# Scores of narrow attention heads on four row strips at once, and a list planner whose passes use eight settings

## The chip, the core and the metric

The kernel runs on one core of one Trainium2 chip. The core has five engines with a queue each: PE (TensorE, the matrix engine; its weight loads are shown apart as PEld), DVE (VectorE), ACT (ScalarE), POOL (GpSimd) and SP (SyncE, which here only issues DMAs). PE writes to PSUM, which has eight banks; DVE and ACT read them. The metric is the device time of one execution in microseconds (us), as the median of several runs.

## The reference, cut to what matters

Four layers run one after another on x, 16 sequences of 128 tokens of width 128, with a context of 16 x 77 tokens of width 96. Each layer is a gated cross attention and a gated feed-forward, both on a normalised x:

```python
x = x + tanh(g_xattn[l]) * xattn_l(layernorm(x), ctx_768)
x = x + tanh(g_ffn[l]) * ffn_l(layernorm(x))
```

The attention of layers 0 and 3 has 16 heads of width 8 (here: the narrow heads):

```python
q = (x @ wq + bq).reshape(B, Sq, 16, 8).transpose(0, 2, 1, 3)
k = (y @ wk + bk).reshape(B, -1, 16, 8).transpose(0, 2, 1, 3)
scores = einsum('bhqd,bhkd->bhqk', q, k) / sqrt(8)
out = einsum('bhqk,bhkd->bhqd', softmax(scores), v)
```

Layer 1 has 16 heads of width 64 (the wide heads), layer 2 one head. The feed-forward of layers 0 and 2 sends each token to two, and to one, of eight experts; that of layer 1 mixes eight linear experts; that of layer 3 has ternary weights.

## The kernel before, in words

**Tiling.** The 16 sequences are four groups of four (GB = 4 batches of a group). Everything is float32; a float32 matmul shows as two passes of PE in a profile, a transpose as one.

**Narrow heads** (`narrow_heads`, line 847). A group gets its keys (a matmul), spreads them with a mask over 128 partitions into `kk`, 32 rows for each strip of four heads, and gets `q` by a projection. Then, for each of four batches: 16 heads are four strips of 32 rows. Two strips write one score tile (`sc_tile`: two PSUM banks), so a batch has two score tiles (`hf` 0 and 1), each from one pair of matmuls of 32 rows by 308 columns. For each tile DVE takes the maximum of each head (`mx_a<-banks`, a reduction) and subtracts it (`shared<-banks,mx_a`), ACT takes the exponential, and PE transposes the result (12 transposes into three banks, copied out by DVE or ACT). Matmuls of 32 columns multiply it with the values; others make the sums, and after four batches the residual x is updated. The values come over DRAM (`all_v`) and are masked on POOL.

**Experts.** After the attention of layers 0 and 2, two groups at a time make a half (`route_half`): DVE ranks the experts, two small matmuls count (`r_seen_f`, `g_sel_f`), DVE computes row indices (`idx_f`), POOL scatters the normalised rows with indirect DMAs (`sorted_x`), SP reads them back in expert order, PE runs the experts tile by tile (`sorted_experts`), and POOL gathers the results (`sorted_y`).

**What sets the order.** No engine's queue is written by hand. Every operation is recorded with an estimated cost, its dependencies and its tiles (`Program.record`); a block `with nc.together(us)` joins several into one operation that is placed as a whole, with all its tiles. `arrange` (line 456) then makes list passes: `forward` takes, step by step, the operation with the smallest start plus weighted cost, under a look-ahead (`ahead`), a weight for old operations (`bias`), a weight of DVE's time (`busy`) and a lead for DMAs (`lead`); `place` gives it PSUM banks and pages and holds back `reserve` of them for older operations; `backward` makes the priorities for the next pass. The pass whose modelled length is shortest is emitted, and each engine executes its part strictly in that order. Copies out of PSUM that either DVE or ACT can make (`nc.either`) get their engine there too. Since all operations are issued from one place, nearly all have line L540 in the profile; tiles tell them apart. `shared` is the common SBUF buffer and `banks` is PSUM.

Of the kernel before, what the change touches and what calls it, by code (L numbers as in the profile page):

```python
# [19 lines left out]
B, S, D = 16, 128, 128  # L20
# [7 lines left out]
PK = 4 * SK  # L28
# [42 lines left out]
class Tile_:  # L71


    def __init__(self, tag, shape, dtype, name, nth):
        self.tag, self.shape, self.dtype, self.name, self.nth = tag, tuple(shape), dtype, name, nth
        self.free = int(np.prod(shape[1:]))
        self.users, self.seen, self.real, self.slot = [], [], None, None
# [135 lines left out]
        self.kept.clear()  # L213


class Program:
    LAG = {"tensor": 0.25, "vector": 0.08, "scalar": 0.08, "gpsimd": 0.1, "sync": 0.1}
    RATE = 290e3
# [2 lines left out]

    PAGE = {"sbuf": 64, "psum": 512}

    def __init__(self, nc, tc, slots, pages, shared, reserve):


        self.nc, self.tc, self.slots, self.reserve = nc, tc, slots, reserve
        self.pages, self.shared = pages, shared
        self.ops, self.count, self.joined, self.shift = [], {}, None, 0
        for e in ("tensor", "vector", "scalar", "gpsimd", "sync"):  # L230
            setattr(self, e, _Engine(self, e))
        self.either = _Engine(self, "vector", "scalar")
        self.spare = _Engine(self, "vector", "gpsimd")
# [219 lines left out]
            op.latest = length - ends[n]  # L453
        return sorted(range(len(ops)), key=lambda n: (-ends[n], n))

    def arrange(self, rounds=7, ahead=800, bias=0.0027, busy=0.33, lead=7.6):

        ops = self.ops
        self.back = [[] for _ in ops]
        for op in ops:  # L460
            for d in op.deps:
                self.back[d].append(op.n)
        order, best = sorted(range(len(ops)), key=lambda n: ops[n].order), None
        for _ in range(rounds):
            length = self.forward(order, ahead, bias, busy, lead)
            if length is None:
                break
            if best is None or length < best[0]:
                places = {t: t.slot for op in ops for t in op.tiles}
                best = length, [(op.start, op.end, op.engine) for op in ops], places  # L470
            order = self.backward()
        assert best is not None, "no room for any tile"
        self.length, times, places = best
        for op, (op.start, op.end, op.engine) in zip(ops, times):
            pass
        for t, t.slot in places.items():
            pass
        return sorted(ops, key=lambda op: (op.start, op.n))
# [116 lines left out]
def tile_gated_blocks(  # L595
# [4 lines left out]
    psum = ctx.enter_context(tc.tile_pool(name="psum", bufs=1, space=PSUM))  # L600

    slots = {
        "mv": 4, "st": 6, "ve": 4, "rstd": 4, "mx": 6, "rs1": 5, "rs2": 4, "off": 4,
    }
# [4 lines left out]
        **{tag: ("sbuf", True) for tag in ("large", "kk", "heads1", "heads2", "we1_sb")},  # L609
    }  # L610
    pages = {"sbuf": 680, "psum": 8}
    nc = Program(tc.nc, tc, slots, pages, shared, {"sbuf": 0, "psum": 1})

    class Tiles:
        def tile(self, shape, dtype=F32, tag=None, name=None):
# [231 lines left out]
    def narrow_heads(layer, wqo, wkv, bq, row, t, groups):  # L847
        for g in groups:
            n = f"a{layer}_{g}"

            mm = mm_tile(f"k_ps_{n}")
            nc.tensor.matmul(mm[:, :GK], lhsT=wkv[: DC + 1, :D], rhs=ctx_of(g), start=True, stop=True)
            kr = sb.tile([P, GB, SK], F32, tag="middle", name=f"kr_{n}")
            evac(kr, mm[:, :GK].rearrange("p (b j) -> p b j", b=GB))
            kk = sb.tile([P, GB, 4, SK], F32, tag="kk", name=f"kk_{n}")
            shape = [P, GB, 4, SK]
            nc.gpsimd.tensor_tensor(
                kk,
                kr[:, :, None, :].to_broadcast(shape),
                col("hmask")[:, None, :, None].to_broadcast(shape),  # L860
                ALU.mult,
            )
            send_narrow_values(g, wkv[: DC + 1, D : 2 * D], n)
            vbs = narrow_values(g, n)
            xnT = transposed(layernorm(g, n), n)
            add_row(g, row)
            q = q_proj(xnT, wqo[:, :D], bq, n)
            oT = sb.tile([P, GB, S], F32, tag="middle", name=f"oT_{n}")
            av, all_chunks = mm_tile(f"av_{n}"), []
            for b in range(GB):  # L870
                scs = [sc_tile(f"sc_{n}_{b}_{hf}") for hf in range(2)]
                for hf in range(2):
                    with nc.together(0.72):
                        for i in range(2):
                            r = 32 * (2 * hf + i)
                            nc.tensor.matmul(
                                scs[hf][:, i, :PK],
                                lhsT=q[r : r + 32, b * S : (b + 1) * S],
                                rhs=kk[r : r + 32, b, :, :].rearrange("p h j -> p (h j)"),
                                start=True,  # L880
                                stop=True,
                            )
                ats, chunks = [], []
                for hf in range(2):
                    scores = scs[hf][:, :, :PK].rearrange("p a (h j) -> p a h j", h=4)
                    at = probabilities(scores, 8, 8.0**-0.5, f"{n}_{b}_{hf}")
                    ats.append(at.rearrange("p r j -> p (r j)"))
                for c in range(3):
                    m = min(CH, PK - c * CH)
                    tp = tp_tile(f"aT_ps_{n}_{b}_{c}")  # L890
                    with nc.together():
                        for k in range(4):
                            at = PK * (k % 2) + c * CH
                            nc.tensor.transpose(tp[:m, k, :], ats[k // 2][:, at : at + m], ident)
                    aT = sb.tile([m, 4, P], F32, tag="middle", name=f"aT_{n}_{b}_{c}")
                    evac(aT, tp[:m])
                    chunks.append(aT)
                avs = av.rearrange("p (b s) -> p b s", b=GB)
                with nc.together(0.8):
                    for c in range(3):  # L900
                        for k in range(4):
                            a = chunks[c][:, k, :]
                            nc.tensor.matmul(
                                avs[32 * k : 32 * k + 32, b, :],
                                lhsT=vbs[b][: a.shape[0], c, k, :], rhs=a,
                                start=(c == 0), stop=(c == 2),
                            )
                all_chunks.append(chunks)


            sums = mm_tile(f"sums_{n}")[:, :S]
            with nc.together(2.6):
                for b in range(GB):
                    for c in range(3):
                        for k in range(4):
                            a = all_chunks[b][c][:, k, :]
                            nc.tensor.matmul(
                                sums[32 * k : 32 * k + 32], lhsT=own[: a.shape[0], c, b, :], rhs=a,
                                start=(b == c == 0), stop=(b == GB - 1 and c == 2),
                            )  # L920
            rs = sb.tile([P, S], F32, tag="rs", name=f"rs_{n}")
            nc.vector.reciprocal(rs, sums)
            wide = mm_tile(f"wide_{n}")
            for b in range(GB):
                nc.tensor.matmul(
                    wide[:, b * S : (b + 1) * S], lhsT=spread[:, b, :], rhs=rs, start=True, stop=True
                )
            rw = sb.tile([P, GT], F32, tag="middle", name=f"rw_{n}")
            evac(rw, wide)
            nc.vector.tensor_tensor(oT.rearrange("p b s -> p (b s)"), av, rw, ALU.mult)  # L930
            y = mm_tile(f"y_{n}")
            with nc.together():
                for b in range(GB):
                    nc.tensor.matmul(
                        y[:, b * D : (b + 1) * D], lhsT=oT[:, b, :], rhs=wqo[:, D : 2 * D],
                        start=True, stop=True,
                    )
            add_to(xs[g].rearrange("p b d -> p (b d)"), y, t)
# [171 lines left out]
    class Route:  # L1110


        def __init__(self, n, count):
            self.n, self.tiles = n, count
            self.e3, self.e4 = [P, count, NE], [P, count, NE, NE]
            self.tri = col("tri").rearrange("p (e f) -> p e f", e=NE)[:, None].to_broadcast(self.e4)
# [678 lines left out]
```

## Time and profile before

| | before |
|---|---|
| median of 3 runs | 726.56 us (726.46 to 730.62) |
| the profiled execution | 725.84 us |
| its span in the profile | 724.0 us |
| mean granted TensorE clock | 0.929 |
| PE, DVE, ACT, POOL busy | 87%, 67%, 55%, 38% of the span |
| passes of the narrow scores (32x308) | 256, busy 40.7 us together |

The profile is one execution. An engine is busy while an instruction of it runs; matmuls overlap in PE's pipeline, so a busy PE is not a full one. A line of a timeline holds merged instructions: start, length, engine, line, operation, output and inputs, count, and in brackets the idle time before and who ended it. "issue" is an idle time for which the profile shows no wait.

### The profile page before, as it was taken

The numbers are of one execution on the slowest core, as the hardware profiler recorded it, in microseconds if no ns is written. First come the engines' busy times: TensorE is split into PE (matmuls) and PEld (weight loads), VectorE is DVE, ScalarE is ACT, GpSimd is POOL, SyncE is SP. The second block draws the span as 40 slices with busy tenths as digits, with TensorE's granted clock in tenths as the row PEclk, the third lists the DMA queues.
The fourth block names the chain that finished last, engine by engine and source line by source line (L and its number), as shares of the span: only waits on it lengthen the run. The fifth ranks groups of instructions, "written<-read, shape, count | busy, mean of one in ns | idle before, by whom it ended". The sixth has DMA issues, their size and how long they took to land. (4 is left out here: it accounts for less than half of the span.)

```text
span 724.0 us, 14843 instructions
## 1 busy us (share of the span) xinstructions
PE 628.8 (87%) x5280; PEld 498.1 (69%) x5280; DVE 483.4 (67%) x1311; ACT 399.3 (55%) x883; POOL 273.9 (38%) x312
## 2 busy tenths in 40 slices
PE   5899477995699989999999999999657998879995
PEld 3587245785698979648756856987434896646795
DVE  5988955582112487398788888737578826587875
ACT  4766224471455587545656466646334664576853
POOL 6524451407104343077274366104646033421010
PEclk9999776998799999999999999999756999979999
DMA  5212530796429776128016437951201932210001
GB/s 136 83 46 80 163 118 16 251 409 256 128 59 340 242 225 195 47 61 232 2 39 181 135 88 250 324 195 36 65 1 55 306 96 60 73 47 14 1 2 59
DMA packets 103239, 92.62 MB, mean 128 GB/s; under 512 B 6726, under 2 KB 92582, under 8 KB 103166
## 3 DMA queue, kind: packets, MB, share of 16 engines
q1 hardware_dynamic: 97166, 81.28, 35.9%
q0 software_dynamic: 3888, 9.35, 4.1%
q10 hardware_dynamic: 2112, 1.05, 0.6%
q8 instruction: 42, 0.69, 0.4%
q14 instruction: 31, 0.25, 0.1%
HBM read 64.29 MB, written 27.36 MB: 127 GB/s over the span
## 5 line engine op out<-in xcount | busy, mean ns | idle before, releaser
L540 PE MATMUL banks<-shared 128*128 128x128 f32 (+8 forms) x3040 | 363.7, 317 | 28.5 <-issue 14.1
L540 PEld LDWEIGHTS banks<-shared 128*128 128x128 f32 (+5 forms) x3040 | 287.3, 174 | 86.0 <-issue 46.0
L540 ACT COPY shared<-banks 104x512 f32<-104x512 f32 (+8 forms) x244 | 142.6, 613 | 126.0 <-PE banks L540 98.7
L540 PE MATMUL banks<-ident,shared 128*128 128x128 f32 (+3 forms) x829 | 124.6, 294 | 32.6 <-DVE shared L540 13.4
L540 PEld LDWEIGHTS banks<-ident,shared 128*128 128x128 f32 (+3 forms) x829 | 100.0, 144 | 62.3 <-issue 18.6
L540 ACT ACTIVATE shared<-banks,shared 128x128 f32<-128x128 f32 x304 | 85.2, 375 | 67.4 <-PE banks L540 37.2
L540 ACT ACTIVATE shared<-shared 128x616 f32<-128x616 f32 (+1 forms) x100 | 70.5, 709 | 59.8 <-DVE shared L540 55.7
L540 DVE TENSOR_TENSOR shared<-banks,shared 128x128 f32<-128x128 f32 (+1 forms) x84 | 26.7, 326 | 85.0 <-PE banks L540 42.2
L540 DVE TENSOR_TENSOR shared<-banks,mx_a 128x616 f32<-128x616 f32 (+1 forms) x100 | 78.1, 781 | 4.2 <-POOL shared L540 0.2
L540 DVE TENSOR_REDUCE mx_a<-banks 128x8 f32<-128x616 f32 (+1 forms) x100 | 77.4, 774 | 5.1 <-PE banks L540 4.0
L540 POOL DMA_INDIRECT sorted_x<-shared,idx_f x48 | 46.7, 974 | 45.7 <-DVE r_both_f L540 22.8
L540 POOL DMA_INDIRECT shared<-sorted_y,idx_f x48 | 46.4, 966 | 45.7 <-DMA sorted_y<-shared 15.0
L540 POOL TENSOR_TENSOR shared<-shared,mine 104x384 f32<-104x384 f32 x32 | 32.5, 1029 | 61.3 <-DMA shared<-all_v 39.7
L540 DVE COPY shared<-banks 128x512 f32<-128x512 f32 (+8 forms) x40 | 25.7, 653 | 40.2 <-PE banks L540 24.0
L540 POOL TENSOR_TENSOR shared<-shared,rs_a 128x616 f32<-128x616 f32 x32 | 38.6, 1217 | 34.7 <-DVE rs_a L540 18.8
L540 POOL TENSOR_TENSOR rstd_f<-ve_f,nhalf 128x4 f32<-128x4 f32 x16 | 16.4, 1022 | 91.0 <-DVE ve_f L540 63.3
L540 POOL TENSOR_TENSOR x<-x,shared 128x128 f32<-128x128 f32 x64 | 28.6, 454 | 39.1 <-DVE x L540 35.3
L540 PE MATMUL banks<-ctx_sb,shared 96*128 96x308 f32 x128 | 38.4, 427 | 0.6 <-DVE x L540 0.6
L540 PE MATMUL banks<-shared,ctx_sb 96*128 96x512 f32 (+1 forms) x80 | 38.4, 596 | 0.2 <-DVE shared L540 0.2
L540 PEld LDWEIGHTS banks<-ctx_sb,shared 96*128 96x128 f32 x128 | 22.3, 190 | 10.3 <-issue 1.9
L540 POOL TENSOR_TENSOR rstd_a<-ve_a,nhalf 128x4 f32<-128x4 f32 x16 | 16.4, 1029 | 31.1 <-DVE ve_a L540 24.3
L540 ACT ACTIVATE shared<-banks,cols_sb 128x128 f32<-128x128 f32 (+1 forms) x44 | 21.3, 521 | 10.7 <-PE banks L540 5.2
(207 smaller groups left out, 665.4 us busy)
## 6 DMA issues: line engine op xcount, KB each, us to landing
shared<-in_wx SPq DMA_DIRECT2D x60, 578.0 KB
shared<-all_u SPq DMA_DIRECT2D x32, 256.0 KB
shared<-all_v SPq DMA_DIRECT2D x32, 156.0 KB
all_v<-shared SPq DMA_DIRECT2D x32, 154.0 KB
sorted_y<-shared SPq DMA_DIRECT2D x76, 64.0 KB
all_u<-shared SPq DMA_DIRECT2D x14, 308.0 KB
shared<-sorted_x SPq DMA_DIRECT2D x6, 512.0 KB
sorted_x<-shared POOLq DMA_DIRECT2D x2, 1472.0 KB
```

Of the source, the lines that this page charges most:

```text
L540: getattr(engine, f)(*(_real(a) for a in args), **done)
```

## The change

It has two parts. The four strips of a batch become one joined operation over both score tiles, with an estimate of 0.8 us instead of twice 0.72; the arithmetic is the same. And the planner's passes take their settings, with the SBUF pages and PSUM banks held in reserve, from a table of eight rows; before, seven passes had one setting and a reserve of no SBUF pages and one PSUM bank.

```diff
+STEPS = [
+    (400, 0.0011, 0.0, 8.6, 30, 2),
+    (400, 0.001, 0.01, 9.2, 30, 2),
+    (300, 0.0041, 0.59, 9.1, 10, 2),
+    (1000, 0.0024, 0.06, 7.8, 0, 3),
+    (1000, 0.0021, 0, 6.2, 0, 3),
+    (1000, 0.0024, 0.08, 6.1, 0, 3),
+    (1000, 0.0021, 0.06, 4.8, 0, 3),
+    (1000, 0.002, 0.01, 6.3, 0, 3),
+]
...
-    def arrange(self, rounds=7, ahead=800, bias=0.0027, busy=0.33, lead=7.6):
+    def arrange(self):
...
-        for _ in range(rounds):
+        for ahead, bias, busy, lead, *pages in STEPS:
+            self.reserve = dict(zip(("sbuf", "psum"), pages))
             length = self.forward(order, ahead, bias, busy, lead)
...
-    nc = Program(tc.nc, tc, slots, pages, shared, {"sbuf": 0, "psum": 1})
+    nc = Program(tc.nc, tc, slots, pages, shared)
...
                 scs = [sc_tile(f"sc_{n}_{b}_{hf}") for hf in range(2)]
-                for hf in range(2):
-                    with nc.together(0.72):
-                        for i in range(2):
-                            r = 32 * (2 * hf + i)
-                            nc.tensor.matmul(
-                                scs[hf][:, i, :PK],
-                                lhsT=q[r : r + 32, b * S : (b + 1) * S],
-                                rhs=kk[r : r + 32, b, :, :].rearrange("p h j -> p (h j)"),
-                                start=True,
-                                stop=True,
-                            )
+                with nc.together(0.8):
+                    for i in range(4):
+                        r = 32 * i
+                        nc.tensor.matmul(
+                            scs[i // 2][:, i % 2, :PK],
+                            lhsT=q[r : r + 32, b * S : (b + 1) * S],
+                            rhs=kk[r : r + 32, b, :, :].rearrange("p h j -> p (h j)"),
+                            start=True,
+                            stop=True,
+                        )
```

Because the planner orders the whole program, both parts move instructions on every engine, in all four layers.

More of the change, by code (lines that the diff above doesn't have):

```diff
@@ L222, with __init__ @@
     PAGE = {"sbuf": 64, "psum": 512}
-    def __init__(self, nc, tc, slots, pages, shared, reserve):
-        self.nc, self.tc, self.slots, self.reserve = nc, tc, slots, reserve
+    def __init__(self, nc, tc, slots, pages, shared):
+        self.nc, self.tc, self.slots = nc, tc, slots
         self.pages, self.shared = pages, shared
```

## The prediction

> **What bounds the kernel now.** The page first: busy shares, then the 40 slices (18.1 us each).
>
> ```profile
> PE 628.8 (87%) x5280; PEld 498.1 (69%) x5280; DVE 483.4 (67%) x1311; ACT 399.3 (55%) x883; POOL 273.9 (38%) x312
> ...
> PE   5899477995699989999999999999657998879995
> ...
> DVE  5988955582112487398788888737578826587875
> ```
>
> PE leads, but its row has holes (slices 5 to 7, 9 to 11, 28 to 31), and where DVE's row shows 8s and 9s early on, PE is not alone. So the second view is busy time by stage:
>
> ```profile
> 0.00:160.00 160.00, 127.41 (x1453) 94.99 (x1454) 117.71 (x284) 82.43 (x161) 65.78 (x76) 0.91 0.43 140
> 160.00:200.00 40.00, 26.14 (x191) 25.76 (x191) 9.60 (x42) 13.40 (x44) 15.40 (x16) 0.79 0.58 204
> 200.00:500.00 300.00, 290.93 (x1841) 231.98 (x1840) 204.56 (x608) 179.85 (x430) 123.13 (x153) 1.00 0.52 158
> 500.00:560.00 60.00, 39.84 (x211) 29.19 (x210) 42.28 (x122) 22.53 (x47) 34.72 (x34) 0.69 0.14 41
> 600.00:724.00 124.00, 104.49 (x1153) 78.62 (x1152) 88.78 (x216) 74.64 (x130) 28.09 (x28) 0.93 0.13 36
> ```
>
> Columns: stretch, its length, PE, PEld, DVE, ACT, POOL busy, granted clock, DMA share, GB/s. From 200 to 500 us PE is busy 97% at full clock: PE work taken out of there shortens the kernel. Layer 0 (0 to 160), the routing for layer 2 (500 to 560) and layer 3 (600 on) are chains in which DVE is busy 70 to 74% and PE waits. The narrow heads, which the change touches, lie only in these.
>
> Third, how the scores run now, in the timeline of PE (start, length, count):
>
> ```profile
> 32.80 0.79 PE L540 MATMUL banks<-shared 32*128 32x308 f32 x4 [0.42 <-DVE shared L540]
> 33.52 0.65 PE L540 MATMUL banks<-ident,shared 128*104 128x128 f32 x4
> ...
> 94.07 0.81 PE L540 MATMUL banks<-shared 32*128 32x308 f32 x8
> 94.81 3.19 PE L540 MATMUL banks<-shared,own 104*32 104x128 f32 x88
> ```
>
> A matmul has two passes here, so x4 is a pair of strips and x8 all four. A lone pair holds PE 0.72 us (32.80 to 33.52), all four strips 0.74 us (94.07 to 94.81). The strips overlap already whenever two pairs stand next to each other.
>
> Fourth, the largest hole, in POOL's and PE's timelines:
>
> ```profile
> 96.25 1.11 POOL L540 DMA_INDIRECT sorted_x<-shared,idx_f  x1 [5.63 <-DVE r_both_f L540]
> ...
> 111.58 0.96 POOL L540 DMA_INDIRECT sorted_x<-shared,idx_f  x1 [0.31 <-issue]
> 126.43 1.04 POOL L540 TENSOR_TENSOR rstd_f<-ve_f,nhalf 128x4 f32<-128x4 f32 x1 [13.89 <-DVE own_f L540]
> ```
>
> ```profile
> 99.73 0.45 PE L540 MATMUL banks<-shared 104*32 104x128 f32 x6 [0.29 <-issue]
> 100.50 0.42 PE L540 MATMUL banks<-shared 104*32 104x128 f32 x4 [0.32 <-issue]
> 101.22 0.31 PE L540 MATMUL banks<-shared 104*32 104x128 f32 x2 [0.29 <-issue]
> ```
>
> While POOL scatters the first half's rows (96 to 112), PE gets a few instructions every 0.7 us and waits for nothing that is shown; from 97.5 to 115.5 PE is busy 9.8 us of 18 and DVE 3.4. The last three scatters then stand behind a normalisation that waits 13.9 us for DVE.
>
> **The change part by part.** Both programs can be built, so I compare their instruction orders. They have the same matmuls and the same POOL and SP instructions; DVE has 16 more, ACT 14 fewer.
>
> *Four strips.* Before, the order holds 21 adjacent foursomes and 22 lone pairs of scores; after, 32 foursomes. By the two rows above PE goes from 21 x 0.74 + 22 x 0.72 = 31.4 us to 32 x 0.74 = 23.7: 7.7 less. 10 of the lone pairs lie in layer 0 and 12 in layer 3. Upper bound of the gain: the scores' row says 40.7 us busy, waits between passes included, so 40.7 - 23.7 = 17. Lower bound: nothing, where DVE ends the wait. I take 2, as PE is 84% busy after 600 us and the 12 there are 12/2 x 0.70 = 4.2.
>
> *Four banks at once.* Both score tiles must now be free (4 of 8 banks) before the foursome starts; before, half a batch could start as soon as one was. Where the next batch waits for the last subtraction of the batch before, DVE idles for PE's start and the foursome: 0.05 us (the pair at 20.98 starts so long after the subtraction's end at 20.93) plus 0.81, say 0.9. There are 31 such changeovers, so at worst 28 us. DVE's new order stands other work between the batches in most: by the mean rows of that work I count 8 changeovers with less than 0.9 us of it, open by 6.2 us together, 3.3 of them in layer 0. Either tile may also come free one subtraction earlier (1.6 us), then nothing is open: bounds 0 and 28, taken 3. Behind the waiting foursome stand, on PE, the transposes of the batch before.
>
> *New order (the list passes).* The planner tries eight settings instead of seven rounds of one, and everything shifts. What the orders show:
>
> PE between the two routings' counting matmuls (159.8 and 541.9 us now): 14 fewer key matmuls of group 0 in the wide layer (two passes of 308 columns, 0.26 us each: six hold PE from 421.23 to 422.78), because they now stand in layer 0's holes: 14 x 2 x 0.26 = 7.3. 8 fewer expert matmuls at 2 x 0.11 (64 passes take 7.36 us) = 1.8, 4 fewer transposes 0.4, one lone pair 0.7: 10.2 us off the stretch that PE bounds for 300 of 382 us. I take 8; bounds 0 (they push out cover there) and 10.
>
> POOL: the normalisation that held three scatters for 13.9 us now stands second, so 15 scatters run in a row, 15 x 1.26 = 19 us after 96 instead of ending at 132. The rows are read at 137.5 now, and PE is 98% busy from 120 to 160 with other work, so this gives little by itself. But group 2's residual is done before the first index, so the whole attention of group 3 and some wide matmuls of 0.26 to 0.43 us, which need fewer instructions per microsecond, are there to fill the hole from 97.5 to 115.5. Between nothing and 14 us (DVE's idle time there); taken 4, because the same scatters run and PE's instructions may come as slowly again.
>
> DVE: the sum of its instructions by their rows grows from 526.6 to 535.1 us, ACT's falls from 465.8 to 458.8 though it loads its tables 22 times instead of 20 (1.28 us each). Ahead of the first index DVE's sums are equal (87.4). The 8 us arise mostly in the wide layers, where DVE is busy 68%: hidden by PE, 0. If that cover is gone, 8.
>
> Tail: after the first score reduction of layer 3's group 2 DVE has 76 us of work instead of 71, but 56 instead of 60 between the last index and that point, and group 0's feed-forward starts 11 us of DVE work earlier. Net 0, bounds -5 and +5.
>
> Sum on the profiled run (725.8 us: span 724.0 and 1.8 around it): -2 + 3 - 8 - 4 = -11, so 714.8; the median of the runs is 0.7 higher, so 715.5, predicted 715.
>
> **The rivals.**
>
> *Nothing to tell.* The foursomes change nothing since most pairs adjoin, and the planner's new order wins in one hole what it loses in another. For it: 7.7 us of PE lie beside DVE work, and total work is the same. Against: the moved key matmuls. 722 to 733, midpoint 727. The Trainium skill, "TensorEngine Tiling (Array Packing)", PSUM Bottleneck, says that a matmul made faster by tiling leaves the reading of PSUM as the bound. By that rule the four strips are worth 0 here and the forecast 717; the rows agree in part: each score tile costs DVE 0.79 + 0.79 us and PE 0.37.
>
> *Slower: the four banks decide.* If foursomes stall PE's queue until both tiles are free, the 6.2 open us are paid, the same again for the 23 covered changeovers at 0.3 each (7), and DVE's extra 8.4 falls on the path in layers 0 and 3; against it stand the 8 of the middle: +14, 740 (734 to 750). It decides once changeovers cost over 0.5 us on average beyond their cover. For it: DVE is busy 19.0 of 20 us from 20 to 40. Against: the fillers. The same page, PSUM Pressure, says that row tiles must lie in different banks and so raise the pressure; no run here yet shows its price.
>
> *Much faster.* The hole at 97.5 closes nearly whole (-13 instead of -4) and the changeovers cost nothing: 703 (698 to 708).
>
> **How the numbers follow.** Forecast (708 to 719) 0.42, much faster 0.16, nothing to tell 0.24, slower 0.18. One per cent, about what can be told from no change, is 7.3 us, so faster means under 719.3 and slower over 733.8: 0.58, 0.24, 0.18. The range 699 to 735 leaves out most of the slower case and the end of the fast one, 0.2 together; the forecast's own range is 708 to 719.
>
> **What would show it.** The scores' row (256 passes) falls from 40.7 us towards 24 to 28, in groups of 8. DVE's reductions show idle time ended by PE: up to 10 us fits, 20 or more is the slower case. The first scatter still starts near 96 and the sixteenth ends near 117. The hole behind it holds more DVE work than 3.4 us. The second counting matmul comes near 158 to 162, the fourth 8 to 12 us before 542; from there to the end it takes 182 as now. I am wrong if the wide layers last as long as now with 14 key matmuls fewer, or if layer 3 lengthens.

## The result and the profile after

| | before | after |
|---|---|---|
| median of 12 runs each | 728.87 us (726.46 to 730.71) | 722.10 us (718.39 to 727.42) |
| the profiled execution | 725.84 us | 722.32 us |
| its span | 724.0 us | 720.6 us |

The ratio is 0.9918, with a 95% interval from 0.9897 to 0.9939: faster by 6.8 us, or 0.8%, where 1.6 to 1.9% was forecast. The direction and the range hold, the size does not.

The page's first rows and the stages of the kernel after (columns as above; the last stretch is 4 us shorter than it was):

```profile
PE 631.9 (88%) x5280; PEld 500.9 (70%) x5280; DVE 492.7 (68%) x1327; ACT 396.9 (55%) x869; POOL 273.2 (38%) x312
...
PE   5989885997599898999999999999648899889987
...
DVE  4998982565023367698888889845488863698775
```

```profile
0.00:160.00 160.00, 132.76 (x1450) 99.17 (x1451) 113.89 (x275) 81.61 (x149) 64.58 (x76) 0.90 0.46 148
...
200.00:500.00 300.00, 290.01 (x1860) 233.93 (x1859) 212.81 (x629) 173.03 (x421) 126.63 (x159) 0.99 0.55 164
```

DVE has 9 us more work, 8 of them in the wide layers, beside a PE that is as full as before. The hole beside the first half's scatters has not closed: in DVE's row slices 6 to 8 were 5, 5, 5 and are 8, 2, 5, so it lies later (slice 7 is 108 to 126 us). PE's timeline has the counting matmuls of the second and the fourth routing:

```profile
166.89 0.34 PE L556 MATMUL banks<-r_seen_f,ones 128*128 128x72 f32 x2
...
540.68 0.70 PE L556 MATMUL banks<-r_seen_f,ones 128*128 128x72 f32 x2 [3.64 <-DVE r_seen_f L556]
```

Before, these stood at 159.8 and 541.9. So layer 0 takes 7.1 us longer, the stretch from the second to the fourth 8.3 us less (373.8 in place of 382.1), and the rest 2.2 us less (179.9 in place of 182.1). The forecast was right about the middle and wrong about layer 0. This is layer 0's hole, in POOL's, DVE's and PE's timelines:

```profile
100.79 1.11 POOL L556 DMA_INDIRECT sorted_x<-shared,idx_f  x1 [2.80 <-DVE st_f L556]
101.93 1.05 POOL L556 TENSOR_TENSOR rstd_f<-ve_f,nhalf 128x4 f32<-128x4 f32 x1
103.18 1.06 POOL L556 DMA_INDIRECT sorted_x<-shared,idx_f  x1 [0.19 <-issue]
...
121.09 0.96 POOL L556 DMA_INDIRECT sorted_x<-shared,idx_f  x1 [0.30 <-issue]
```

```profile
113.70 0.28 DVE L556 TENSOR_SCALAR bos<-bos,tg 128x128 f32<-128x128 f32 x1
124.54 0.22 DVE L556 COPY gs_f<-banks 128x64 f32<-128x64 f32 x1 [10.57 <-remote]
```

```profile
112.86 0.96 PE L556 MATMUL banks<-route,shared 128*128 128x16 f32 x8
113.76 1.61 PE L556 MATMUL banks<-shared 32*128 32x308 f32 x8
117.81 1.29 PE L556 MATMUL banks<-shared 32*128 32x308 f32 x4 [2.44 <-ACT shared L556]
124.82 1.39 PE L556 MATMUL banks<-shared 32*128 32x308 f32 x4 [5.72 <-DVE gs_f L556]
```

The copy of `gs_f` reads what the `route` matmuls wrote, and these end at 113.8 by PE's rows, yet it starts 10.7 us later, 2.5 us after the last scatter (122.05). "remote" says that the view names no one who released it. PE in its turn waits for DVE with the second half of a foursome. In the kernel before, DVE's last wait there likewise ended 2.4 us after a run of scatters (the run's end at 112.5, then this copy):

```profile
114.95 1.29 DVE L540 COPY shared<-banks 104x512 f32<-104x512 f32 x2 [7.71 <-remote]
```

The trace also records semaphores, the counters by which one engine tells another that it is done. The copy of `gs_f` waits for PE's counter, which rises at 116.72 us and then four times from 124.45 to 124.59. Matched in order, these four belong to matmuls that by PE's rows ended at 113.82 (the last `route` one) to 115.37; without the scatters (below) the same four rises come within 0.1 us of the matmuls' ends. In the kernel before, four rises from 114.87 to 115.04 belong to matmuls that ended from 106.2 to 111.6. So, as far as the match goes, DVE and ACT stand because PE's signals come late, here by up to 10.6 us. It is not complete: of the 17 rises due from 99.6 to 115.4 us three have no record.

The scores' rows, the reductions' before and after and PE's after (busy, mean ns, idle before and who ended it):

```profile
L540 DVE TENSOR_REDUCE mx_a<-banks 128x8 f32<-128x616 f32 (+1 forms) x100 | 77.4, 774 | 5.1 <-PE banks L540 4.0
L556 DVE TENSOR_REDUCE mx_a<-banks 128x8 f32<-128x616 f32 (+1 forms) x100 | 77.4, 774 | 9.9 <-PE banks L556 8.7
```

```profile
L556 PE MATMUL banks<-shared 32*128 32x308 f32 x256 | 35.0, 508 | 11.5 <-DVE gs_f L556 5.7 <-ACT shared L556 3.7 <-DVE shared L556 2.0
```

PE's fell from 40.7 to 35.0, not towards 24 to 28. Passes that wait in the hole count too, but they are the smaller part: without the scatters the row is 32.4. The reductions' idle time ended by PE rose from 4.0 to 8.7.

### The profile page after: what moved, and what is told of

It is laid out like the page before. It is cut to its first block, busy times and chain, and to the rows that moved or that the text cites. A ratio compares the mean times of both kernels' runs of the same rounds, so it can differ in the third digit from the quotient of the medians.

```text
span 720.6 us, 14909 instructions
## 1 busy us (share of the span) xinstructions
PE 631.9 (88%) x5280; PEld 500.9 (70%) x5280; DVE 492.7 (68%) x1327; ACT 396.9 (55%) x869; POOL 273.2 (38%) x312
## 5 line engine op out<-in xcount | busy, mean ns | idle before, releaser
L556 PE MATMUL banks<-shared 128*128 128x128 f32 (+7 forms) x3040 | 366.6, 323 | 53.6 <-issue 15.6
L556 PEld LDWEIGHTS banks<-shared 128*128 128x128 f32 (+4 forms) x3040 | 287.7, 177 | 115.0 <-issue 48.4
L556 ACT COPY shared<-banks 104x512 f32<-104x512 f32 (+9 forms) x234 | 137.5, 610 | 133.5 <-PE banks L556 116.8
L556 PE MATMUL banks<-ident,shared 128*128 128x128 f32 (+3 forms) x829 | 123.0, 295 | 11.7 <-ACT shared L733 3.6
L556 PEld LDWEIGHTS banks<-ident,shared 128*128 128x128 f32 (+3 forms) x829 | 101.0, 146 | 41.4 <-issue 14.5
L556 POOL TENSOR_TENSOR rstd_f<-ve_f,nhalf 128x4 f32<-128x4 f32 x16 | 16.4, 1024 | 134.2 <-DVE ve_f L556 94.1
L556 DVE COPY shared<-banks 104x512 f32<-104x512 f32 (+10 forms) x50 | 33.7, 680 | 26.3 <-PE banks L556 22.2
L556 PE MATMUL banks<-shared,ctx_sb 96*128 96x512 f32 (+1 forms) x80 | 40.9, 632 | 0.1
L556 PE MATMUL banks<-ctx_sb,shared 96*128 96x308 f32 x128 | 36.9, 425 | 0.0
```

The lines of the kernel that those rows point to most:

```text
L556: getattr(engine, f)(*(_real(a) for a in args), **done)
```

## The experiments

Theory after the result: the middle's gain is the moved key matmuls; layer 0 lost because the run of scatters holds the other engines up, whatever work stands ready. Rivals: four banks at once do it; or one of the change's two parts does all. All ratios are against the kernel before, run beside (728.5 to 732.4 us).

**The two parts alone.** First the foursomes with the old seven passes, then the eight settings with the old pairs.

```diff
 strips only:   the kernel before
-                for hf in range(2): with nc.together(0.72): two strips
+                with nc.together(0.8): four strips
 settings only: the kernel after
-                with nc.together(0.8): four strips
+                for hf in range(2): with nc.together(0.72): two strips
```

> The kernel before with the foursomes alone; the planner keeps its seven passes of one setting and its old reserve. My theory is that the strips by themselves are worth at most the 2 us that I gave them, and that a changed order decides the rest: 724 to 734 us against about 729 for the kernel before, the scores' row at 26 to 32 us. If the strips carry the change's gain (rival), about 722. If four banks at once stall the queue of PE (rival), the reductions of the scores show 20 us or more of idle time ended by PE, and the time is 735 or more.

> The kernel after with two pairs of strips in place of each foursome; the planner keeps its eight settings. If the settings bring the gain (theory): 718 to 726 us, and from the second to the fourth counting matmul some 376 us as after the change, or less. If the strips bring it (rival): about 729.

Strips alone: 753.93 us, ratio 1.0328 (1.0271 to 1.0385). Settings alone: 737.81, 1.0130 (1.0070 to 1.0189). The stretch from the second to the fourth counting matmul takes 385 us with the settings alone, not the 376 that I expected. Both are slower than before, and both parts together are faster: there is no gain of a part to be added up, since each variant is a new order of the whole program. The first shows 20.2 us of reductions' idle time ended by PE, which is what I had written down for four banks that stall PE; the split foursomes below speak against that cause, though in another order, so what makes this order slow stays open.

**Without the scatters.** In each kernel's own order, the 16 scatters of layer 0's first half are left out when the program is emitted, so that this half's expert rows stay zero.

```diff
+                op = nc.gpsimd.indirect_dma_start(...)
+                if n == "f0_0":
+                    op.calls.clear()
```

> The kernel after in its own order, without the 16 scatters of layer 0's first half (the expert rows of that half stay zero, so two of the four groups get no expert output from their own rows); every other instruction stands where it stood. If the scatters hold the other engines up (theory), the idle time of 10.6 us before the copy of gs_f goes, the granted clock stays above 0.8 between 100 and 125 us, layer 0 ends 8 to 12 us earlier and the time is 710 to 715 us. If the hole is a chain of the order itself (rival), it stays, and the time is 720 to 724.

> The kernel before in its own order, without the same 16 scatters (the expert rows of layer 0's first half stay zero). If the scatters hold the other engines up (theory): from 97.5 to 115.5 us PE is busy 15 us or more in place of 9.8, and the time falls by 6 to 12 us, to 717 to 723. If both kernels lose the same to the scatters, the difference between this and the kernel after without scatters stays at 7 us; if the kernel after loses more to them, it is 10 or more. Rival, the hole is the order's own: no change, 729.

After without them: 705.82 us, 0.9666 (0.9616 to 0.9716). Before without them: 708.22, 0.9713 (0.9662 to 0.9764). Both gain more than I expected: 16 and 21 us. The stage of the hole, before with and then without scatters (two traces, columns as above):

```profile
96.00:121.00 25.00, 16.66 (x171) 10.01 (x164) 8.82 (x16) 3.93 (x7) 12.63 (x13) 0.66 0.12 41
```

```profile
96.00:121.00 25.00, 24.64 (x474) 21.78 (x471) 19.52 (x50) 12.45 (x23) 2.04 (x2) 1.00 0.34 120
```

The same order, with the same work ready: PE issues 474 passes in place of 171, DVE works 19.5 us in place of 8.8, and the granted clock is 1.00 in place of 0.66. The hole is not the order's. Where the steps come in time (us, one profile each):

| | before | after | before, no scatters | after, no scatters |
|---|---|---|---|---|
| index of half 0 | 95.8 | 100.4 | 96.0 | 100.6 |
| x of group 3 | 138.8 | 146.9 | 123.0 | 133.4 |
| index of half 1 | 163.1 | 170.3 | 147.3 | 156.7 |
| index of layer 2's half 1 | 546.1 | 546.1 | 526.3 | 532.2 |

By these profiles the scatters cost 15.8 us before and 13.6 after up to half 1's index, and without them the new order is 9.4 us later there: layer 0 is longer by itself. Single profiles of one order differ: with plain DMAs in place of the scatters (below) half 1's index of the order after comes at 154.4 and 152.6. So layer 0 is longer by 5 to 9 us, and the stall costs 14 to 18 us after, about as much as before.

**Foursomes apart.** The order after; the second pair of nearly every foursome is issued one PE step later.

```diff
+                if four is not None:          # a foursome
+                    for call in [*late, *op.calls[:2]]:
+                        call(engine)
+                    late, tile = op.calls[2:], four
+                    continue
...
+                if late and op.engine == "tensor":
+                    for call in late:
+                        call(engine)
```

> The kernel after in its own order, but the second pair of strips of nearly every foursome is issued one step of PE later (27 of 32 foursomes become two lone pairs; all else stands as it stood). By the rows of 0.72 us for a lone pair and 0.74 for a foursome this gives PE 27 x 0.70 = 19 us more. My theory, that foursomes save PE time beside work of DVE: 722 to 727 us. If the strips are on the path (rival): 732 or more. If four banks at once hold PE up (rival), lone pairs are faster: 715 to 720, and the reductions' idle time ended by PE falls below the 8.7 us of the kernel after.

738.52 us, 1.0163 (1.0101 to 1.0225), 16.4 above the kernel after: 0.61 us for each of 27 pairs of strips taken apart. PE's row of the scores grows from 35.0 to 54.6 us. Against my theory, the strips are on the path. The reductions now wait more for PE, not less:

```profile
L571 DVE TENSOR_REDUCE mx_a<-banks 128x8 f32<-128x616 f32 (+1 forms) x100 | 77.5, 775 | 17.3 <-PE banks L571 14.8
```

So whatever it costs to need four banks at once, in this order it is less than taking the foursomes apart costs.

**What of a scatter it is.** The same 64 KB each, as plain DMAs from POOL, then from SP.

```diff
+                if n == "f0_0":
+                    op.calls[:] = [lambda engine: engine.dma_start(out=d.rows[at : at + P], in_=xn[:, i, :])]
```

> The kernel after in its own order; the 16 scatters of layer 0's first half become 16 plain DMAs of the same 64 KB from the same queue of POOL (rows go to fixed places, so that half's rows reach the wrong experts). Leaving the scatters out took 16 us. If writing descriptors on POOL is what holds the others up, the hole stays: 718 to 724. If it is the scatter with indices alone, it goes: 706 to 711.

> As the run before, but the 16 plain DMAs stand in the queue of SP. If POOL's part of a scatter holds the others up (theory): the hole goes, 706 to 711 us. If it is the traffic itself (1 MB in 128 pieces of 512 B each), it stays: 718 to 724.

706.95 us (0.9714, 0.9659 to 0.9770) and 708.20 (0.9733, 0.9683 to 0.9783): as without scatters. Neither the megabyte (16 times 128 rows of 512 B) nor POOL's queue does it by itself. What is left is the form with indices, or the long run that it makes: plain ones follow each other every 0.5 us, so that theirs is short.

```profile
100.64 8.03 POOL L1397 DMA_DIRECT2D sorted_x<-shared  x15
```

**Pauses between scatters.** The order after, with a small operation on POOL behind each scatter (first a power of 1.02 us behind all 16, then behind every second, then a short multiplication behind all, then a power behind every fourth); the short one also in the kernel before.

```diff
+                if n == "f0_0":               # or: and k, for every second
+                    op.calls.append(
+                        lambda engine: engine.tensor_tensor(pad[:, :4], pad[:, 4:], pad[:, 4:], ALU.pow)
+                    )
```

> The kernel after with its scatters, but POOL does a small power of 128x4 (1.02 us in the row of rstd_f) after each of the 16 scatters of layer 0's first half, so that they come every 2.4 us in place of 1.27, and end near 140 us. Nothing of the result changes. If the stall comes from scatters that follow each other without a pause, DVE's idle time of 10.6 us before the copy of gs_f falls below 4 and the time is 712 to 719; if each scatter holds the others up by a fixed time (16 us / 16 = 1 us), the hole is only spread, 719 to 725; if the later rows are what matters, 725 or more.

> The kernel after with a 1 us power on POOL after every second scatter of layer 0's first half: the sixteenth ends near 132 us in place of 140 as with 16 powers, so that rstd_f of group 3 and the reading of the rows should not come late. Theory (scatters one after the other without a pause stall PE): if pairs of scatters are still harmless, x3 is updated near 135 us, the second index comes near 159 and the time is 708 to 714. If every pair of scatters already stalls (rival), x3 is updated at 141 or later and the time is 716 to 722.

> The kernel after with a short multiplication (128x128, 0.46 us by the row of x<-x,shared) on POOL after each of the 16 scatters: one every 1.75 us, the sixteenth near 131 us. If a pause of half a microsecond is enough: 708 to 714 us, x3 updated near 135. If the stall goes with the rate of scatters (rival; 1.27 us stalls, 2.3 does not): 714 to 720, x3 near 140.

> The kernel after with a 1 us power after every fourth scatter of layer 0's first half (four powers). If the stall builds up over a long run of scatters without a pause: runs of four are still short, x3 is updated near 133 us and the time is 707 to 712. If it goes with the mean rate (1.27 us stalls, 1.75 does not; here 1.53): x3 at 137 to 142 and 712 to 718.

> The kernel before with the same short multiplication after each scatter of layer 0's first half. There rstd_f of group 2 stands behind thirteen scatters and will come near 119 us; without stalls its inputs are there at 108. If the scatters' rate is what stalls: x2 is updated near 110 to 114 us instead of 123.7, and the time is 718 to 725; the gain is smaller than in the kernel after, whose rstd_f stands second. If pauses do nothing (rival): 728 to 732.

| | us | ratio (95%) | x of group 3 |
|---|---|---|---|
| all 16, 1.02 us | 719.51 | 0.9857 (0.9789 to 0.9925) | 135.0 |
| every second, 1.02 us | 709.39 | 0.9708 (0.9669 to 0.9748) | 133.2 |
| all 16, short | 710.94 | 0.9725 (0.9689 to 0.9761) | 135.1 |
| every fourth, 1.02 us | 711.07 | 0.9734 (0.9701 to 0.9767) | 135.3 |
| before, all 16, short | 720.32 | 0.9856 (0.9817 to 0.9895) | 131.8 |

In the kernel after each pattern brings group 3's x to within 2 us of where it comes without any scatter (133.4), though all scatters are done. POOL and DVE with a pause after every second:

```profile
102.65 0.98 POOL L558 DMA_INDIRECT sorted_x<-shared,idx_f  x1 [0.30 <-issue]
103.65 1.04 POOL L1397 TENSOR_TENSOR pad<-pad 128x4 f32<-128x4 f32 x1
104.89 1.03 POOL L558 DMA_INDIRECT sorted_x<-shared,idx_f  x1 [0.20 <-issue]
```

```profile
111.07 0.22 DVE L558 COPY gs_f<-banks 128x64 f32<-128x64 f32 x1 [0.77 <-PE banks L558]
```

The 10.57 us before the copy are 0.77. With all sixteen long pauses the hole goes as well, but the scatters end at 140 us: DVE then waits 4.06 us for group 3's `rstd_f`, which stands behind them on POOL, and the rows are read 12 us later than in the kernel after (141.65 for 130.03), so the gain is paid back. Runs of four with a pause behind them are nearly harmless there, which fits a stall that builds up over a longer run. In the kernel before, x of group 2 comes at 112.3 us in place of 123.7, and then POOL's queue shows what it waits for:

```profile
117.71 1.01 POOL L542 DMA_INDIRECT sorted_x<-shared,idx_f  x1 [0.17 <-issue]
118.74 0.42 POOL L1382 TENSOR_TENSOR pad<-pad 128x128 f32<-128x128 f32 x1
119.10 1.06 POOL L542 TENSOR_TENSOR rstd_f<-ve_f,nhalf 128x4 f32<-128x4 f32 x1
```

`rstd_f` of group 2 runs with no idle time before it, behind the thirteenth scatter, 6.8 us after that x; without scatters it runs 2.8 us after it (108.6 and 111.4). In the kernel after it stands second.

**The moved key matmuls.** The 14 key matmuls of the wide layer that the new order puts into layer 0 are left out.

```diff
+                if getattr(op, "key", False) and not second:   # wide group 0, before half 1's index
+                    continue
```

> The kernel after in its own order, without the 14 key matmuls of the wide layer's group 0 that stand in layer 0 (28 passes, 7.3 us by 0.26 us a pass; group 0 of layer 1 gets other keys). My prediction had them stand in holes, where they cost nothing: then the second half's index comes at 170.6 us as now and the time stays at 720 to 724. If they are on the path (theory now, since PE is busy 95% between the two indices when the scatters are away): the index comes 4 to 7 us earlier and the time is 715 to 718.

724.45 us, 0.9902 (0.9865 to 0.9940), and half 1's index at 170.7: nothing is gained. In layer 0, with its stall in place, they cost nothing; my new theory fell, and the prediction's reading was right there. Without the stall it was not tried.

**Is the strips' price a by-product of the stall?** Foursomes apart, with a pause after every second scatter.

> The kernel after with the pauses of the run with one power after every second scatter, and with the second pair of nearly every foursome one step later, as in the run with the foursomes apart. There, 27 foursomes apart cost 16 us (0.6 each). If that price is PE's own (27 x 0.70 = 19 us, most of it on the path): again 12 to 16 us above the 709 of the kernel with pauses, 721 to 726. If it came from the stall behind the scatters: 709 to 716.

729.89 us, 0.9993 (0.9962 to 1.0023): 20.5 above the 709.39 with foursomes, 0.76 us a pair and more than the 12 to 16 expected. So the price does not come from the stall; it fits the 0.70 us of PE.

**All runs of scatters.** A power after every second scatter in both halves of layer 0 (`n[:2] == "f0" and k`), then also in layer 2 (`(i * top + k) % 2`).

> The kernel after with a 1 us power after every second scatter in both halves of layer 0. The second half's scatters run while PE waits for little else (165 to 185 us: PE 5.3 us of 10 busy). If they stall PE there too, the time falls below 709 by 3 to 8 us: 701 to 706. If the rows are waited for (rival), the 8 pauses come on top: 712 to 718.

> As before, but with a power after every second scatter in layer 2's two halves as well (8 scatters each, 420 and 547 us). At 420 PE runs long matmuls and shows no gaps, at 547 its gaps lie within a chain of DVE: I expect no change against the run with both halves of layer 0, within 3 us; if these stalls count too (rival), 4 us or more less.

694.09 us, 0.9507 (0.9471 to 0.9544): the best version, faster than both kernels and with the whole result. Pauses in layer 2 as well gain nothing more (696.26, 0.9544, 0.9511 to 0.9578). The stretch of the first run of scatters, and 10 us from the middle of the second, in the kernel after and then in this one, where the second run starts 11 us earlier (159.4 for 170.7):

```profile
100.00:125.00 25.00, 13.87 (x76) 9.61 (x76) 11.91 (x35) 8.64 (x16) 16.78 (x17) 0.72 0.12 42
180.00:190.00 10.00, 4.68 (x24) 4.49 (x24) 0.29 (x1) 0.00 (x0) 7.56 (x9) 0.67 0.34 109
```

```profile
100.00:125.00 25.00, 20.36 (x175) 14.82 (x177) 20.24 (x50) 14.43 (x25) 20.93 (x20) 0.86 0.40 148
170.00:180.00 10.00, 10.00 (x92) 10.00 (x91) 2.27 (x7) 6.55 (x22) 8.55 (x9) 1.00 0.91 296
```

While the second half is scattered, PE goes from 4.7 busy us of 10 to all 10, at full clock.

**The change without the stall.** A power after every fourth scatter of both halves, in both kernels.

> The kernel before with a 1 us power on POOL after every fourth scatter in both halves of layer 0 (four powers each). If the stall belongs to the scatters and not to one order: x2 is updated near 110 us in place of 123.7, the 20 us after the second index lose their gaps too, and the time is 692 to 704. If runs of four still stall where short instructions stand (rival): 705 to 715.

> The kernel after with the same powers. The first half kept 711 us with every fourth against 709 with every second; with both halves 694 is known for every second, so 692 to 698. Against the run before it, this is the change itself without the stall: if the new order's gain in the wide layers (7 us) and the strips outweigh the 9 us that layer 0 loses without scatters, it is 2 to 6 us faster than the kernel before with powers; if not, the two are equal within 2 us.

Before: 711.99 us (0.9742, 0.9702 to 0.9782). After: 697.48 (0.9538, 0.9493 to 0.9584). With pauses the change is worth 14.5 us, not 2 to 6; with half 0's scatters left out it was 2.4 (708.22 and 705.82). The two don't measure the same: runs of four still hold the old order up, which has more and shorter instructions there. This is the old order with them, to be read against its two rows above:

```profile
96.00:121.00 25.00, 20.00 (x252) 16.18 (x246) 14.31 (x31) 9.49 (x16) 18.09 (x18) 0.86 0.13 42
```

PE issues 252 passes, between the 171 with all scatters in one run and the 474 with none, and half 1's index comes at 157.4 us, not at 147.3. So how much the change is worth, from 2 to 15 us, depends on how hard the scatters hit each of the two orders; what they do to the chip was in none of my terms. Pauses after every second scatter were not tried in the old order, so its best time is open.

## Why the prediction was right in the middle and wrong in layer 0

- **The step that failed is the new order in layer 0**, forecast as a gain ("taken 4, because the same scatters run and PE's instructions may come as slowly again"). Layer 0 got 7.1 us longer. Two things in that step were wrong.
- **The hole was misread.** I took it as room that the attention of group 3 would fill in part. It is a stall: while the scatters run one behind the other, ready work doesn't run either. It cost 15.8 us before and 14 to 18 after, so at most 2.2 of the 4 came, and within the spread of these profiles perhaps nothing. That a mechanism like this was at work stood in the rows that I showed ("issue" every 0.7 us); what it costs was not to be had from them, and I bounded only how much of it might be filled.
- **Most of the miss is a term that I put at nothing.** Without the stall layer 0 of the new order is 5 to 9 us longer by itself. Hence the points that failed with it: first scatter near 96 (100.8), sixteenth's end near 117 (122.05), second counting matmul at 158 to 162 (166.9), and the fourth 8 to 12 us before 542 (540.7). I had compared DVE's sums ahead of the first index (equal) and not the order on the path to it. Up to that index DVE is now busy 82.0 us of 100.4, before 80.3 of 95.8: 1.7 us more work and 2.9 more idle time. And DVE's timeline shows the update of x and three of four groups of statistics between the index's last reduction and its conversion.

```profile
98.24 0.21 DVE L556 TENSOR_REDUCE r_both_f<-r_row_f 128x8 f32<-128x64 f32 x1
98.36 0.74 DVE L556 SCALAR_TENSOR_TENSOR x<-banks,tg,x 128x512 f32<-128x512 f32 x1
...
100.35 0.14 DVE L556 CAST idx_f<-r_last_f 128x8 int32<-128x8 f32 x1
```

  That is some 2 of the 4.6 us by which the first index is late. The rest, and what is lost between the first index and the second, I have not taken apart: why the new order is longer there stays open.
- **The middle was right in size.** Taken 8, measured 8.3 between the second and the fourth counting matmul. That it is the moved key matmuls fits but is not shown, and some of the agreement is luck: without half 0's scatters the stretch between the last two rows of the table of steps is only 3.5 us shorter in the new order (375.5 for 379.0), where with them it is 7.2 (375.8 for 383.0). That the key matmuls are free in layer 0, beside the stall, is shown by leaving them out. DVE's extra 9 us are hidden there, as predicted.
- **Four strips were mis-sized.** Taken 2 of 7.7; a pair apart costs 0.61 to 0.76 us in the order after, so by my estimate the 11 more foursomes are worth some 7 to 8 us there: 11 x 0.61 = 6.7, 11 x 0.76 = 8.4. The Trainium skill ("TensorEngine Tiling (Array Packing)", PSUM Bottleneck) says only that copies out of PSUM "may become" the bottleneck after a fourfold speedup; the rule that I made of it, that the strips gain nothing, does not hold here. But the price belongs to an order: strips alone, in an order that the old passes made for them, lose 25 us.
- **Four banks at once** were taken as 3. No run isolates their cost; as the foursomes apart are slower, the rival "four banks decide" is out for this order. **The tail** gained 2.2 us where I had 0, within its 5.
- Sum by my stages, on the profiled runs: layer 0 some -3 forecast (with all of the strips' -2 and the banks' +3 put there), +7.1 measured; middle -8 and -8.3; tail 0 and -2.2. That is -3.4 of span for -11; the medians, of 12 runs each, give -6.8.

## What to carry to other kernels

When an engine's timeline shows small bursts and idle time that no one ends, beside a run of DMAs with indices, take that run out once in the old order before counting on the hole as room for other work. A pause in a run, or other work of POOL put between its members, can be worth more than a new order (13 us here for eight idle operations of 1 us in one run, 28 us for sixteen in two) and less where something that others wait for stands behind the run on that queue, since pauses make the run longer (sixteen long ones left 719.51). And where a planner orders everything, two parts of a change can't be priced apart: price each at a fixed order.

## What the runs showed of the hardware

- A run of 16 scatters with indices on POOL, one each 1.27 us, holds PE, DVE and ACT up; plain DMAs of the same bytes from the same queue don't, and runs of four with 1 us behind them hardly do in the kernel after. In both kernels the stall ends about 2.4 us after the run. PE's signals arrive up to 10.6 us after the modelled ends of their matmuls in it, and four late ones then come within 0.2 us. The Trainium skill ("SBUF — State Buffer", Who interferes with whom) says that a DMA never contends with a compute engine. Here a run of scatters costs 14 to 18 us, and the measurement decides; the page speaks of SBUF's ports, and no run shows that these are what is short. What holds the signals back stays open, also whether the recording of the profile, some of whose records are missing there, has a part in it.
- Late fetches of instructions are not seen: in the kernel before, one 16 KB fetch falls into the run (at 108.65 us) and takes 0.96 us, where the others of its queue take 0.9 to 1.5.
- The granted clock falls with the stall: it is 0.72 from 100 to 125 us in the kernel after and 0.67 from 180 to 190; in the matching stretches of the best version it is 0.86 and 1.00, and over the whole span 0.953 in place of 0.923.
